# Convolution first, turned copies on GpSimd, and a projection by halves of a chunk, in a four-layer network of scans

## The chip, the cores and the metric

The kernel runs on one core of a Trainium2 chip. The core has a matrix engine (TensorE, PE in the profile; its weight loads are PEld), VectorE (DVE), ScalarE (ACT), GpSimd (POOL) and SyncE (SP, which here only issues DMAs). The metric is the device time of one execution in microseconds. A time "before" is the median of three runs.

## The reference

Four layers, each `x = x + layer(groupnorm(x))` on an image batch of 4 x 64 x 64 x 192 in float32. Layers 0 and 3 are the ones touched. Both are a two-dimensional selective scan; layer 0 has 384 inner channels (DI), layer 3 has 192. Cut to what matters (layer 0):

```python
xz = x @ in_proj_w.T
xp, z = (xz[..., :DI], xz[..., DI:])
xc = silu(depthwise_conv3x3(xp, conv_w) + conv_b)      # channels first, 64 x 64
x0 = xc.reshape(B, DI, L)                              # read by rows, L = 4096
x1 = jnp.swapaxes(xc, 2, 3).reshape(B, DI, L)          # read by columns
xs = jnp.stack([x0, x1, x0[..., ::-1], x1[..., ::-1]], axis=1)
x_dbl = jnp.einsum('bkdl,kcd->bkcl', xs, x_proj_weight)   # 44 rows: 12 step, 16 B, 16 C
dts = jnp.einsum('bkrl,kdr->bkdl', dts_r, dt_projs_weight)
delta = jax.nn.softplus(dts + dt_projs_bias[None, :, :, None])

def step(h, inp):
    u_l, dt_l, Bl, Cl = inp
    dA = jnp.exp(dt_l[..., None] * A[None])
    h = dA * h + (dt_l * u_l)[..., None] * Bl[:, :, None, :]
    y = jnp.sum(h * Cl[:, :, None, :], axis=-1)
    return (h, y)
```

Layer 1 holds four one-dimensional scans along lines of the image, layer 2 a Toeplitz product. The four directions of a scan are added, normalized, gated with `silu(z)` and projected back.

## The kernel before

Layers 0 and 3 run image by image. For each image there are three stages, in pools of memory of their own: `ss2d_input`, `ss2d_scan`, `ss2d_output`.

`ss2d_input` (L430) normalizes the image, then goes through NT tiles of P channels (3 of 128 in layer 0, 2 of 96 in layer 3). For each tile TensorE makes the input projection (`in_ps`, 8 chunks of 512 pixels, L455) and ScalarE copies it into a zero-framed image `pad` (L459). The 3 x 3 convolution follows. For the last tile it is nine TensorE matmuls per chunk with diagonal weights `taps` into `conv_ps` (L472), and ScalarE applies the silu twice, into `o` by rows (L473) and into `by_col` by columns (L474). For the other tiles it is nine VectorE operations on the whole tile (L481, L483), and ScalarE again applies the silu twice (L484, L485). Each tile is stored whole, `o` to `u_d[0]` and `by_col` to `u_d[1]` (L487). There are four PSUM tiles for `in_ps` and `conv_ps`, two buffers of `o` and one of `by_col`.

`ss2d_scan` (L489) takes 32 jobs for an image: four directions of 8 chunks of 512 pixels. A job has units of 64 channels by 4 of the 16 states (two states on each half of the partitions): 24 units in layer 0. `run_jobs` (L104) writes out the order of the units. The preparation of later jobs is put between the units of the running one, at offsets in units that the table `when` gives (L513): load u at -33, project at -29, turn_b at -27, step_size at -21, -19, -17, finish at -15, turn at -13, -11, -9. These steps are in `prepare` (L189):

- `project`: `xd_ps`, three matmuls that add up the 44 rows x 512 (L199), the copy `xd` (L201) and its store to `bc_dram` (L211), from which rows of B and C are read back broadcast.
- `turn_b`: the 16 rows of B turned in four pieces (`b_ps`, L219), copied to `bt` (L221), from which ScalarE makes the diagonal tiles `diag` (L282).
- `step_size(t)`: one matmul with 12 rows of contraction for each tile of 128 channels (`dt_ps`, L225), copied out with a bias into `delta` (L228).
- `finish`: softplus (L232), then on VectorE `dtu` = delta x u (L233). `turn`: `dtu` turned (L242).

The PSUM pool `mm` that these steps use has two tiles of one bank each. A unit has: on TensorE `b` (eight matmuls of 64 x 256, L324), on ScalarE two exponentials `dA` (L347), on VectorE two scans of 512 (L364), on ScalarE a copy of the carried state (L367), on GpSimd the product `hc` with C (L369), and on TensorE the sum over states `y` (two matmuls of 64 x 512, L387). Three units of a job in layer 0 are "direct": their b comes from GpSimd (`bs`, L301) and TensorE makes none. `b` has two PSUM buffers.

The program's order on each engine is settled when it is built, by a scheduler that may move an instruction past others; each engine then runs its list in order, and waits on semaphores. SP issues nearly all DMAs in one list.

Of the kernel before, what the change touches and what calls it, by code (L numbers as in the profile page):

```python
# [7 lines left out]
F32 = mybir.dt.float32  # L8
AF = mybir.ActivationFunctionType
# [4 lines left out]
B, HW, L = 4, 64, 4096  # L14
C = 192
PC, KC = 96, 2
N = 16
R = 12
E = R + 2 * N
T = 512  # L20
NCH = L // T
ROWS = T // HW
PAIRS = N // 4
NB = T // 128
# [12 lines left out]
class Kernel:  # L37
# [151 lines left out]
    def prepare(self, job, pools):  # L189

        nc = self.nc
        prep, mm = pools["prep"], pools["mm"]
        P, NT, DI, w = job["P"], job["NT"], job["DI"], job["w"]

        def project():
            u = job["u"]
            ps = mm.tile([E, T], F32, name="xd_ps", tag="mm")
            for t in range(NT):
                nc.tensor.matmul(ps, w["xw"][:, t, :], u[:, t], start=t == 0, stop=t == NT - 1)  # L199
            xd = job["xd"] = prep.tile([E, T], F32, name="xd", bufs=1)  # L200
            nc.scalar.copy(xd, ps)  # L201
            job["bc"] = self.bcd.tile([2 * N, T], F32, name="bc_dram")
            if job["carry"] is None:

                by_half = job["bc"].rearrange("(a n) l -> a (n l)", n=2).rearrange(
                    "a (h n l) -> h a n l", h=2, n=2
                )
                for h in range(2):
                    nc.scalar.dma_start(by_half[h], xd[0 : 2 * N, h * 256 : (h + 1) * 256])
            else:  # L210
                nc.scalar.dma_start(job["bc"], xd[0 : 2 * N, :])  # L211
            job["delta"] = prep.tile([P, NT, T], F32, name="delta", bufs=1)
            job["dtu"] = prep.tile([P, NT, T], F32, name="dtu", bufs=1)
            job["dtuT"] = prep.tile([128, NB, DI], F32, name="dtuT",)

        def turn_b():
            ps = mm.tile([128, NB, N], F32, name="b_ps", tag="mm")
            for k in range(NB):
                nc.tensor.transpose(ps[:, k, :], job["xd"][0:N, k * 128 : (k + 1) * 128], self.ident[:N, :N])  # L219
            bt = job["bt"] = prep.tile([128, NB, N], F32, name="bt")  # L220
            nc.scalar.copy(bt, ps)  # L221

        def step_size(t):
            dp = mm.tile([P, T], F32, name="dt_ps", tag="mm")
            nc.tensor.matmul(  # L225
                dp, w["dtw"][2 * N : E, t * P : (t + 1) * P], job["xd"][2 * N : E, :], start=True, stop=True
            )
            nc.scalar.activation(job["delta"][:, t, :], dp, AF.Identity, bias=w["dtb"][:, t : t + 1])  # L228
# [201 lines left out]
    def ss2d_input(self, x_in, xn_d, u_d, P, NT, inw, cw, cb):  # L430

        tc, nc = self.tc, self.nc
        S = HW + 2
        with (
# [16 lines left out]
            for t in range(NT):  # L451
                for c in range(NCH):
                    ps = psum.tile([P, T], F32, name="in_ps", tag="mm")
# [6 lines left out]
                        pad[:, t, 1 + c * ROWS : 1 + (c + 1) * ROWS, 1 : 1 + HW],  # L460
                        ps.rearrange("p (a b) -> p a b", b=HW),
                    )
                o = pu.tile([P, HW, HW], F32, name="o")
                by_col = pu.tile([P, HW, HW], F32, name="by_col", bufs=1)
                bias = cb[:, t : t + 1]
                if t == NT - 1:
                    for c in range(NCH):
                        rows = slice(c * ROWS, (c + 1) * ROWS)
                        ps = psum.tile([P, ROWS, HW], F32, name="conv_ps", tag="mm")
                        for j in range(9):  # L470
                            win = pad[:, t, c * ROWS + j // 3 : (c + 1) * ROWS + j // 3, j % 3 : j % 3 + HW]
                            nc.tensor.matmul(ps, taps[:, j, :], win, start=j == 0, stop=j == 8)  # L472
                        nc.scalar.activation(o[:, rows, :], ps, AF.Silu, bias=bias)  # L473
                        nc.scalar.activation(  # L474
                            by_col.rearrange("p b a -> p a b")[:, rows, :], ps, AF.Silu, bias=bias
                        )
                else:
                    for j in range(9):
                        win = pad[:, t, j // 3 : j // 3 + HW, j % 3 : j % 3 + HW]
                        if j == 0:  # L480
                            nc.vector.tensor_scalar_mul(o, win, cw[:, t, 0:1])  # L481
                        else:
                            nc.vector.scalar_tensor_tensor(o, win, cw[:, t, j : j + 1], o, ALU.mult, ALU.add)  # L483
                    nc.scalar.activation(by_col.rearrange("p b a -> p a b"), o, AF.Silu, bias=bias)  # L484
                    nc.scalar.activation(o, o, AF.Silu, bias=bias)  # L485
                for to, of in zip(u_d, (o, by_col)):
                    nc.sync.dma_start(to[:, t, :], of.rearrange("p a b -> p (a b)"))  # L487

    def ss2d_scan(self, pre, u_d, y_d, P, NT, ways, A, dtb):  # L489
        tc, nc, ins = self.tc, self.nc, self.i  # L490
        DI = P * NT
        bufs = dict(c=5, bc=2, diag=5, both=6, dtu2=2) if NT == 3 else dict(c=6, bc=2, diag=6, both=6, dtu2=4)
        with (
# [27 lines left out]
            for k, (col, rev) in sorted(enumerate(ways), key=lambda one: one[1]):  # L521
                w = {"dtb": dtb[:, k, :], "A": A[:, k]}

                def weights(k=k, w=w):
                    w["xw"] = self.load(pw, "xw", ins[f"{pre}x_w"][k])
                    w["dtw"] = pw.tile([E, DI], F32, name="dtw")
                    nc.sync.dma_start(w["dtw"][2 * N : E, :], ins[f"{pre}dt_w"][k])

                for c in range(NCH - 1, -1, -1) if rev else range(NCH):
                    first = not jobs or jobs[-1]["k"] != k  # L530
# [575 lines left out]
```

## Time and profile before

| | |
|---|---|
| median of three runs | 31847.99 us (31831.84 to 31864.97) |
| profiled execution | 31794.9 us, span 31793.1 us |
| PE busy | 28311.3 us (89%) |
| ACT busy | 23362.1 us (73%) |
| POOL busy | 22678.0 us (71%) |
| DVE busy | 22474.8 us (71%) |
| mean granted TensorE clock | 0.948 |
| scans of layer 0, image 0 (from first scan to last) | about 229 to 2530 us |
| input stage of layer 0, image 0 (to the first `xd_ps`) | 0 to 191.6 us |

Layer 0 takes the first 10.8 ms; layer 3 begins at about 25.3 ms. In the lines of the timeline the columns are start, duration, engine, line, operation, result<-operands, shapes and count, and in brackets how long the engine stood idle before it and what ended that. A group of instructions has after the bar its busy time, the mean of one in ns, and the idle time before it with the releasers. A line of busy time by stretch gives the stretch, its length, and for each engine the busy time and the number of instructions.

### The profile page before, as it was taken

How to read it: one execution, taken by the hardware profiler on the slowest of the kernel's cores; microseconds unless marked ns; L12 is line 12 of the kernel's file. 1: busy time of each engine (PE TensorE's matmuls, PEld its weight loads, DVE VectorE, ACT ScalarE, POOL GpSimd, SP SyncE). 2: the span in 40 equal slices, each digit the busy share in tenths (PEclk: the TensorE clock that was granted, in tenths of full speed). 3: DMA queues.
4: the chain of work that ended last, by engine and by line, in shares of the span. 5: the costliest groups of instructions: out<-in, count | busy, mean ns of one | idle time of the engine just before them, and what ended most of it. 6: DMA issues, size and time to landing. Idle time of an engine off the chain costs nothing. (4 is left out here: it accounts for less than half of the span.)

```text
span 31793.1 us, 449637 instructions
## 1 busy us (share of the span) xinstructions
PE 28311.3 (89%) x162840; PEld 13772.2 (43%) x162840; DVE 22474.8 (71%) x16587; ACT 23362.1 (73%) x50239; POOL 22678.0 (71%) x9755
## 2 busy tenths in 40 slices
PE   8997998999899699999999999999588988888888
PEld 4453554454445344444444444444355343434344
DVE  7887887788788677777777777777433267676767
ACT  7885885887688488888888888888133287878788
POOL 6884885888488488888888888888000086767777
PEclk9998999999999899999999999999788999999999
DMA  3333333333333423233333333333533444444444
GB/s 101 100 97 110 99 97 107 103 98 98 109 100 97 135 93 93 93 97 98 98 98 96 95 95 95 98 98 99 132 72 72 109 129 120 128 124 125 124 124 124
DMA packets 1565670, 3326.87 MB, mean 105 GB/s; under 512 B 343781, under 2 KB 356438, under 8 KB 1546934
## 3 DMA queue, kind: packets, MB, share of 16 engines
q1 hardware_dynamic: 1403702, 3021.19, 34.7%
q10 hardware_dynamic: 159744, 276.91, 2.6%
q8 instruction: 1289, 21.12, 0.3%
q14 instruction: 935, 7.66, 0.1%
HBM read 2137.94 MB, written 656.08 MB: 88 GB/s over the span
## 5 line engine op out<-in xcount | busy, mean ns | idle before, releaser
L369 POOL TENSOR_TENSOR hc<-h,c 128x1024 f32<-128x1024 f32 x7680 | 18189.2, 2384 | 3115.9 <-DVE h L364 1317.7
L324 PE MATMUL b<-diag,dtuT 128*64 128x256 f32 x98304 | 12805.9, 391 | 800.1 <-DVE h L364 679.9
L324 PEld LDWEIGHTS b<-diag,dtuT 128*64 128x64 f32 x98304 | 7507.3, 140 | 6835.9 <-issue 3091.1
L387 PE MATMUL y<-hc,fold 128*64 128x512 f32 x30720 | 8995.0, 598 | 587.4 <-POOL hc L369 572.6
L364 DVE TENSOR_TENSOR_SCAN h<-dA,carry,b 128x512 f32<-128x512 f32 x6720 | 8195.0, 1264 | 1805.9 <-PE b L324 1134.3
L347 ACT ACTIVATE dA<-both,A 128x512 f32<-128x512 f32 (+1 forms) x12288 | 8279.8, 711 | 203.0 <-DVE h L357 182.0
L357 DVE TENSOR_TENSOR_SCAN h<-dA,b 128x1024 f32<-128x1024 f32 x2304 | 5251.7, 2284 | 2047.7 <-PE b L324 883.2
L282 ACT ACTIVATE diag<-ident,bt 128x128 f32<-128x128 f32 x20480 | 6527.3, 391 | 124.5 <-ACT b L347 86.1
L301 POOL TENSOR_TENSOR bs<-dtu,bc 128x1024 f32<-128x1024 f32 x1536 | 3638.4, 2369 | 1479.7 <-DMA c<-bc_dram 1087.9
L387 PEld LDWEIGHTS y<-hc,fold 128*64 128x64 f32 x30720 | 2497.6, 138 | 2981.7 <-POOL hc L369 1262.0
L441 POOL MEMSET pad<- 128x13068 f32 (+1 forms) x8 | 73.4, 9177 | 3977.5 <-DMA inw<-in_L_in_w 3004.7
L347 ACT ACTIVATE b<-both,A 128x504 f32<-128x504 f32 (+1 forms) x3072 | 2078.1, 676 | 412.7 <-DVE h L364 379.8
L357 DVE TENSOR_TENSOR_SCAN h<-b,bs 128x1024 f32<-128x1024 f32 x768 | 1754.1, 2284 | 659.6 <-ACT b L347 391.2
L367 ACT COPY carry<-h 128x2 f32<-128x2 f32 x4608 | 851.4, 185 | 1367.1 <-DVE h L364 1165.5
L364 DVE TENSOR_TENSOR_SCAN h<-b,carry,bs 128x512 f32<-128x512 f32 x1344 | 1638.0, 1259 | 105.7 <-POOL hc L369 95.3
L364 DVE TENSOR_TENSOR_SCAN h<-dA,b 128x512 f32<-128x512 f32 x960 | 1112.9, 1205 | 436.2 <-ACT dA L347 175.8
L347 ACT ACT_TABLE_LOAD x1018 | 1306.1, 1283 | 15.0 <-ACT b L335 0.3
L730 PE MATMUL in_ps<-xn,in_w 96*128 96x512 f32 x1536 | 933.4, 738 | 329.4 <-DMA xn<-m_row 177.8
L747 DVE SCALAR_TENSOR_TENSOR u<-in_ps,conv_w,u 128x504 f32<-128x504 f32 (+2 forms) x1152 | 835.7, 725 | 460.3 <-ACT u L742 438.6
L233 DVE TENSOR_TENSOR dtu<-delta,u 128x1536 f32<-128x1536 f32 (+1 forms) x256 | 611.4, 2388 | 758.2 <-ACT delta L232 602.9
L242 PEld LDWEIGHTS dtu_ps<-ident,dtu 128*128 128x128 f32 (+1 forms) x4096 | 422.1, 142 | 875.7 <-issue 569.3
L730 PE MATMUL z_ps<-xn,in_w 96*128 96x512 f32 x1536 | 761.7, 618 | 0.0
(155 smaller groups left out, 22077.8 us busy)
## 6 DMA issues: line engine op xcount, KB each, us to landing
c<-bc_dram SPq DMA_DIRECT2D x3072, 256.0 KB
both<-delta SPq DMA_DIRECT2D x2048, 128.0 KB
bc<-bc_dram SPq DMA_DIRECT2D x768, 256.0 KB
both<-delta_dram SPq DMA_DIRECT2D x768, 256.0 KB
dtu<-dtu_dram SPq DMA_DIRECT2D x768, 256.0 KB
dtu<-dtu SPq DMA_DIRECT2D x1280, 128.0 KB
L_y<-out ACTq DMA_DIRECT2D x512, 256.0 KB
u<-L_u SPq DMA_DIRECT2D x160, 768.0 KB
```

The costliest lines, as they stand in the source:

```text
L233: (nc.gpsimd if job["carry"] is None else nc.vector).tensor_mul(job["dtu"], delta, job["u"])
L282: nc.scalar.activation(to, self.ident, AF.Copy, scale=of)
L301: self.nc.gpsimd.tensor_mul(by(b), dtu, by(job["bbc"][p]))
L324: nc.tensor.matmul(to, job["dtuT"][:, k, g * 64 : (g + 1) * 64], job["diag"][p][:, k, 2 * q : 2 * q + 2, :], start=True, stop=True,)
L347: nc.scalar.activation(to[n], of, AF.Exp, scale=w["A"][:, g, 2 * p + n : 2 * p + n + 1])
L357: nc.vector.tensor_tensor_scan(h[:, way], dA[:, way], b[:, way], 0.0, ALU.mult, ALU.add)
L364: nc.vector.tensor_tensor_scan(hn[:, n, way], dA[:, n, way], by_n[:, n, way], start, ALU.mult, ALU.add)
L367: nc.scalar.copy(carry[g, p], hn[:, :, 0 if rev else T - 1])
L369: nc.gpsimd.tensor_mul(hc, h, job["cbc"][p])
L387: nc.tensor.matmul(y[c * 64 : (c + 1) * 64, :], self.fold, of, start=first == 0 and n == 0, stop=last == LAST and n == 1)
L730: nc.tensor.matmul(ps, w["in_w"][:, k, to + t * P : to + (t + 1) * P], job["xn"][:, k, :], start=k == 0, stop=k == KC - 1,)
L747: nc.vector.scalar_tensor_tensor(u[:, :, to], ps[:, :, of], tap(3 - j), u[:, :, to], ALU.mult, ALU.add)
```

## The change

In `ss2d_input` the loop over tiles is split: first all input projections and copies into `pad`, then the convolutions, beginning with the last tile, TensorE's. ScalarE now applies the silu once; the copy by columns is made from its result by GpSimd. In TensorE's tile each chunk goes to a small tile `one` and is stored by itself; in the others the first chunk (8 rows) is finished and stored ahead of the rest. `by_col` has two buffers.

In `prepare`, for jobs of layer 0 alone (`halves`), `project` computes the two halves of a chunk's 512 pixels on two halves of the output rows (0-43 and 64-107), so that `xd` is 128 x 256; the 44 columns of the weights are filled up with zeros to 64. `bc_dram` is written by two DMAs; `turn_b` turns two pieces of 128 x 128; `step_size` makes two matmuls of 256 pixels, from rows 32-43 and from rows 96-107, into two PSUM tiles, each copied out by itself. For this the weights of `dt` are loaded twice, at two row positions, and `xw` gets a memset on GpSimd, in layer 3 too.

```diff
+        halves = job["carry"] is not None and NT == 3
         def project():
             u = job["u"]
-            ps = mm.tile([E, T], F32, name="xd_ps", tag="mm")
-            for t in range(NT):
-                nc.tensor.matmul(ps, w["xw"][:, t, :], u[:, t], start=t == 0, stop=t == NT - 1)
-            xd = job["xd"] = prep.tile([E, T], F32, name="xd", bufs=1)
+            if halves:
+                ps = mm.tile([128, 256], F32, name="xd_ps", tag="mm")
+                for t in range(NT):
+                    for h in range(2):
+                        nc.tensor.matmul(
+                            ps[h * 64 : (h + 1) * 64, :], w["xw"][:, t, :], u[:, t, h * 256 : (h + 1) * 256],
+                            start=t == 0, stop=t == NT - 1,
+                        )
+                xd = job["xd"] = prep.tile([128, 256], F32, name="xd", bufs=1)
...
+            elif halves:
+                by_half = job["bc"].rearrange("a (h l) -> h a l", h=2)
+                for h in range(2):
+                    nc.scalar.dma_start(by_half[h], xd[h * 64 : h * 64 + 2 * N, :])
...
         def turn_b():
+            if halves:
+                ps = mm.tile([128, 2, 128], F32, name="b_ps", tag="mm")
+                for k in range(2):
+                    nc.tensor.transpose(ps[:, k, :], job["xd"][:, k * 128 : (k + 1) * 128], self.ident)
+                of = ps.rearrange("p k (h e) -> p k h e", h=2)[:, :, :, 0:N]
+                nc.scalar.copy(bt.rearrange("p (h k) n -> p k h n", h=2), of)
+                return
...
         def step_size(t):
+            if halves:
+                parts = []
+                for h in range(2):
+                    parts.append(mm.tile([P, 256], F32, name="dt_ps", tag="mm"))
+                    rows = slice(h * 64 + 2 * N, h * 64 + E)
+                    nc.tensor.matmul(
+                        parts[h], w["dtw"][rows, t * P : (t + 1) * P], job["xd"][rows, :], start=True, stop=True
+                    )
+                for h in range(2):
+                    to = job["delta"][:, t, h * 256 : (h + 1) * 256]
+                    nc.scalar.activation(to, parts[h], AF.Identity, bias=w["dtb"][:, t : t + 1])
+                return
...
-                o = pu.tile([P, HW, HW], F32, name="o")
-                by_col = pu.tile([P, HW, HW], F32, name="by_col", bufs=1)
+            for t in [NT - 1, *range(NT - 1)]:
+                by_col = pu.tile([P, HW, HW], F32, name="by_col")
+                turned = by_col.rearrange("p b a -> p a b")
                 bias = cb[:, t : t + 1]
...
-                        nc.scalar.activation(o[:, rows, :], ps, AF.Silu, bias=bias)
-                        nc.scalar.activation(
-                            by_col.rearrange("p b a -> p a b")[:, rows, :], ps, AF.Silu, bias=bias
-                        )
+                        one = pu.tile([P, ROWS, HW], F32, name="one")
+                        nc.scalar.activation(one, ps, AF.Silu, bias=bias)
+                        nc.gpsimd.tensor_copy(turned[:, rows, :], one)
+                        nc.sync.dma_start(u_d[0][:, t, c * T : (c + 1) * T], one.rearrange("p a b -> p (a b)"))
...
-                    nc.scalar.activation(by_col.rearrange("p b a -> p a b"), o, AF.Silu, bias=bias)
-                    nc.scalar.activation(o, o, AF.Silu, bias=bias)
-                for to, of in zip(u_d, (o, by_col)):
-                    nc.sync.dma_start(to[:, t, :], of.rearrange("p a b -> p (a b)"))
+                    for rows in (slice(0, ROWS), slice(ROWS, HW)):
+                        nc.scalar.activation(o[:, rows, :], o[:, rows, :], AF.Silu, bias=bias)
+                        nc.sync.dma_start(
+                            u_d[0][:, t, rows.start * HW : rows.stop * HW],
+                            o[:, rows, :].rearrange("p a b -> p (a b)"),
+                        )
+                    nc.gpsimd.tensor_copy(turned, o)
+                nc.sync.dma_start(u_d[1][:, t, :], by_col.rearrange("p a b -> p (a b)"))
...
-                    w["xw"] = self.load(pw, "xw", ins[f"{pre}x_w"][k])
-                    w["dtw"] = pw.tile([E, DI], F32, name="dtw")
-                    nc.sync.dma_start(w["dtw"][2 * N : E, :], ins[f"{pre}dt_w"][k])
+                    w["xw"] = pw.tile([P, NT, 64], F32, name="xw")
+                    nc.gpsimd.memset(w["xw"][:, :, E:64], 0.0)
+                    nc.sync.dma_start(w["xw"][:, :, 0:E], ins[f"{pre}x_w"][k])
+                    w["dtw"] = pw.tile([128, DI], F32, name="dtw")
+                    for h in range(2):
+                        nc.sync.dma_start(w["dtw"][h * 64 + 2 * N : h * 64 + E, :], ins[f"{pre}dt_w"][k])
```

In the built program the order on each engine stays as it was for layers 1 and 2. In an input stage of layer 0 ScalarE's list is now: the 24 copies into `pad`, three chunks of the last tile, tile 0, three chunks, tile 1, two chunks. SP's list ends with the turned tile 1, the last chunk, the turned last tile, the weights and u.

More of the change, by code (lines that the diff above doesn't have):

```diff
@@ L193, in prepare @@
         P, NT, DI, w = job["P"], job["NT"], job["DI"], job["w"]
+        halves = job["carry"] is not None and NT == 3
         def project():
             u = job["u"]
-            ps = mm.tile([E, T], F32, name="xd_ps", tag="mm")
-            for t in range(NT):
-                nc.tensor.matmul(ps, w["xw"][:, t, :], u[:, t], start=t == 0, stop=t == NT - 1)
-            xd = job["xd"] = prep.tile([E, T], F32, name="xd", bufs=1)
+            if halves:
[7 more added lines that the diff above has]
+                xd = job["xd"] = prep.tile([128, 256], F32, name="xd", bufs=1)
+            else:
+                ps = mm.tile([E, T], F32, name="xd_ps", tag="mm")
+                for t in range(NT):
+                    nc.tensor.matmul(ps, w["xw"][:, t, 0:E], u[:, t], start=t == 0, stop=t == NT - 1)
+                xd = job["xd"] = prep.tile([E, T], F32, name="xd", bufs=1)
             nc.scalar.copy(xd, ps)
@@ L216, in turn_b @@
         def turn_b():
+            bt = job["bt"] = prep.tile([128, NB, N], F32, name="bt")
+            if halves:
[5 more added lines that the diff above has]
+                return
             ps = mm.tile([128, NB, N], F32, name="b_ps", tag="mm")
@@ L219, in turn_b @@
                 nc.tensor.transpose(ps[:, k, :], job["xd"][0:N, k * 128 : (k + 1) * 128], self.ident[:N, :N])
-            bt = job["bt"] = prep.tile([128, NB, N], F32, name="bt")
             nc.scalar.copy(bt, ps)
         def step_size(t):
+            if halves:
[10 more added lines that the diff above has]
+                return
             dp = mm.tile([P, T], F32, name="dt_ps", tag="mm")
@@ L472, in ss2d_input @@
                             nc.tensor.matmul(ps, taps[:, j, :], win, start=j == 0, stop=j == 8)
-                        nc.scalar.activation(o[:, rows, :], ps, AF.Silu, bias=bias)
-                        nc.scalar.activation(
-                            by_col.rearrange("p b a -> p a b")[:, rows, :], ps, AF.Silu, bias=bias
-                        )
+                        one = pu.tile([P, ROWS, HW], F32, name="one")
+                        nc.scalar.activation(one, ps, AF.Silu, bias=bias)
+                        nc.gpsimd.tensor_copy(turned[:, rows, :], one)
+                        nc.sync.dma_start(u_d[0][:, t, c * T : (c + 1) * T], one.rearrange("p a b -> p (a b)"))
                 else:
+                    o = pu.tile([P, HW, HW], F32, name="o")
                     for j in range(9):
```

## Prediction

> **What bounds the kernel now.** I read four views: busy time by stretch, to see which engine fills the scans of layer 0; groups of instructions in 500 to 2300 us (25 chunks of image 0), for counts and durations; the timeline of TensorE in one chunk, for what a step costs in place; and the timelines of ScalarE and TensorE through an input stage.
>
> Busy time by stretch:
>
> ```profile
> core 0: us, PE busy (x) PEld busy (x) DVE busy (x) ACT busy (x) POOL busy (x), PEclk, DMA share, GB/s
> 500.00:2300.00 1800.00, 1698.44 (x11440) 900.24 (x11438) 1536.32 (x1257) 1505.62 (x3692) 1578.72 (x673) 0.97 0.38 99
> ```
>
> Per chunk (divide by 25): 72.0 us, with TensorE 67.9 busy, GpSimd 63.1, VectorE 61.5, ScalarE 60.2. TensorE is the bound; the next engine has 8.9 us to spare. Its missing 4.1 us come once a chunk:
>
> ```profile
> L324 PE MATMUL b<-diag,dtuT 128*64 128x256 f32 x8356 | 1079.1, 393 | 101.6 <-DVE h L364 101.4
> L233 DVE TENSOR_TENSOR dtu<-delta,u 128x1536 f32<-128x1536 f32 x25 | 76.8, 3072 | 27.0 <-ACT delta L232 27.0
> ```
>
> 101.6 / 25 = 4.1 us of waiting for the scans: VectorE puts the 3.07 us product dtu between two scans, after 1.1 us of waiting for delta, and both PSUM buffers of b are then full.
>
> What a step costs, in place:
>
> ```profile
> 1224.51 1.89 PE L387 MATMUL y<-hc,fold 128*64 128x512 f32 x8
> 1226.23 2.31 PE L199 MATMUL xd_ps<-u,xw 128*44 128x512 f32 x5
> ...
> 1251.58 1.06 PE L387 MATMUL y<-hc,fold 128*64 128x512 f32 x4
> 1252.44 1.93 PE L324 MATMUL b<-diag,dtuT 128*64 128x256 f32 x16
> 1254.16 1.06 PE L387 MATMUL y<-hc,fold 128*64 128x512 f32 x4
> 1255.15 1.12 PE L225 MATMUL dt_ps<-xd,dtw 12*128 12x512 f32 x2
> 1256.20 1.95 PE L324 MATMUL b<-diag,dtuT 128*64 128x256 f32 x16
> 1257.98 1.03 PE L387 MATMUL y<-hc,fold 128*64 128x512 f32 x4
> ```
>
> A float32 matmul is two records. From start to start, eight products of b (256 columns each, in pairs on output rows 0-63 and 64-127) take 1.72 us, 0.43 a pair; two y (512 columns) take 0.86 together. So two halves of the output rows run at once. The projection xd has one half only: three matmuls of 512 columns at 0.86 are 2.58 us. One dt matmul takes 0.99 + 1.05 + 1.78 less the undisturbed 0.86 + 1.72 = 1.24 us, 0.86 of it streaming and 0.38 the change to and from its shape.
>
> The input stage of image 0:
>
> ```profile
> 78.13 31.07 PE L472 MATMUL conv_ps<-pad,taps 128*128 128x512 f32 x72
> 141.91 33.21 PE L472 MATMUL conv_ps<-pad,taps 128*128 128x512 f32 x72 [32.71 <-ACT by_col L474]
> 191.61 5.32 PE L199 MATMUL xd_ps<-u,xw 128*44 128x512 f32 x6 [16.49 <-DMA u<-L_u]
> ...
> 109.27 7.46 ACT L484 ACTIVATE by_col<-o,cb 128x4096 f32<-128x4096 f32 x1 [29.05 <-DVE o L483]
> 127.22 7.19 ACT L484 ACTIVATE by_col<-o,cb 128x4096 f32<-128x4096 f32 x1 [6.76 <-DVE o L483]
> ```
>
> The convolution on TensorE is half done at 109.2, then stands for 32.7 us: four PSUM tiles are full, and ScalarE waits in order for VectorE and writes the turned copies (7.2 to 7.5 us each, 3.7 for the straight ones). After it ends, 16.5 us pass until u has been stored and loaded.
>
> **What the Trainium skill says.** "TensorEngine Tiling (Array Packing)", Key Properties: tiles of the array run independently, while a change of tiling mode drains it. The trace agrees on both: 0.43 us for a pair, and 0.38 us around a dt step. "TensorE: Matmul & The Clock Gate", Why this matters for your kernels: contractions of few rows placed in different row groups run concurrently (four tiles measured 3.07 times faster). In this trace only a hint: at 197.73 a matmul of b_ps (rows 0-15) and at 197.74 one of dt_ps (rows 32-43) start together. "GPSIMD Engine Reference", 8. Key points: GpSimd shares its SBUF interfaces with VectorE when VectorE reads two SBUF inputs. The trace agrees: dtu takes 1.76 us at 204.89 with GpSimd idle, 3.07 beside it.
>
> **The change, part by part.**
>
> *xd by halves* (layer 0, 4 images x 32 = 128 chunks). Three matmuls become six of 64x256 in pairs, the shape of b: 3 x 0.43 = 1.29 instead of 2.58. Saved: 1.29 us of TensorE per chunk.
>
> *b_ps.* Four turns of 16 rows cost 0.49 in place (start of b_ps 1234.07, b 1234.41, plus 0.15 around). Two of 128x128: four such (dtu) cost 0.74 in place, 0.43 of it streaming, so two cost 0.52. Nothing either way.
>
> *dt by halves.* Per step, two matmuls of 256 columns in row groups 32 and 96, to two PSUM tiles. If concurrent, 0.43 + 0.38 instead of 1.24: 0.43 saved, three times a chunk: 1.29. If serial, 0. I take concurrent, on the page and the hint.
>
> *ScalarE.* Each dt leaves two evictions of 256 instead of one of 512. Between 0.39 (128 columns) and 0.67 (512) I take 0.45 each: +0.23 x 3 = +0.7; the copy of xd falls from 0.56 to about 0.4; one DMA issue more (0.33 us, beside other work in the trace). ScalarE goes from 60.2 to about 61, hidden in a period near 70. But the last dt eviction stands before the softplus that dtu waits for: +0.25 us, and in the built order a copy of carry, which waits for a scan, stands between its halves. I charge 0.4 us a chunk (0 to 0.8), which lengthens the stall of TensorE.
>
> Each dt step now fills both tiles of the pool mm. Evictions follow their matmul by about 1.7 to 2.2 us (1255.15 to 1257.33) and the next user comes 6.4 us later: no wait.
>
> Scan: 1.29 + 1.29 - 0.4 = 2.2 us x 128 = 282 us. Nothing else is late before that: a period of 69.8 stands above GpSimd's 63.1 and VectorE's 61.5.
>
> *Input stage, layer 0.* With ScalarE only emptying PSUM between, TensorE runs on: 72 products x 0.86 from 78.1 end at 140.0, the last silu at 140.7. VectorE's convolutions end at 127.2 and now have GpSimd's copies beside them, 7168 elements by then. A copy is not in the trace: at least the memset's rate (13068 in 10.99 us, 0.84 ns), at most that of the product hc (1024 in 2.37, 2.3 ns). So 6 to 16 us of GpSimd, of which VectorE loses part; I take 4 (0 to 16): 131. Then silu of this tile, 4 us, 135; its turned copy 5.5 us (3.4 to 9.4), 140.5; the last chunk's copy, 142. SP has in order the 2 MB store of this turned tile, the last chunk, the 2 MB store of the last turned tile, the weights (one DMA more each, 0.4), then u at about 143.5. The stores ran at 419 GB/s: 5 us each, from 140.5 to 150.7, then u with 0.8 MB and about 2 us of latency: xd at about 155 instead of 191.6. I take 36 us saved, 21 (copy and contention at their worst) to 42 (u not queued behind the stores). Times 4: 144.
>
> *Input stage, layer 3.* There TensorE is in front too: its convolution starts at 27004.81, waits 11.8, and xd comes at 27097.8, 9 us of that waiting for the last whole-tile store. Unbroken it ends at 27066.6; silu, copy, a 1.6 MB store (3.8 us) and u lead to about 27077. Saved 20 us (15 to 24), times 4: 80. Layer 3's scan keeps its matmuls; its weights gain a memset and one small DMA, long before use.
>
> Layers 1 and 2 have the same instructions in the same order.
>
> Sum: 282 + 144 + 80 = 506 us. Against the profiled execution (31794.9): 31289. The median of the runs is 53 us above that one, so 31848 - 506 = 31342.
>
> **Rivals.**
> 1. *Row groups do not overlap for float32.* For it: yt_ps uses two quadrants at once and still takes 21.4 us for 192 products of 64 columns, 0.11 each, which is serial streaming (or the rate of issue). Against: the hint above. Scan 0.9 x 128 = 115: 115 + 224 = 339, 31509.
> 2. *Another engine sets the scan.* GpSimd has direct units with two products (4.74 us) in a row, and VectorE catches up only where TensorE has extra work, which is what goes. Then only the input stages gain: 31848 - 224 = 31624. Against: 6 to 8 us of slack a chunk.
> 3. *The input stages give nothing,* because turned copies, VectorE's slowdown and 4 MB of stores end as late as before. It needs about 36 us of delay in each: 31848 - 282 = 31566.
> 4. *Slower.* TensorE, in order, waits in each dt step for both tiles of mm to be emptied, since ScalarE waits for scans between. At one unit (2.6 us) a step, 7.8 - 2.6 = 5.2 us a chunk, x 128 = 666, less 224: 32290. It decides above a stall of 1.6 us a step (224/128 = 1.75, plus 2.6 of gain, plus the 0.5 of the bound below, over 3). The built order puts evictions close behind, which speaks against.
>
> **How the numbers follow.** Forecast 0.52; rivals 1 to 4: 0.20, 0.10, 0.06, 0.12. The likeliest's own range is 31255 to 31440. For 8 in 10 it must reach over rivals 1 and 3 and the edge of 2: 31250 to 31610. About 64 us (0.2%) is what a measurement can tell from no change. Rivals 1 to 3 are all faster; of rival 4 I put 0.10 beyond 64 us slower and 0.02 within, so faster 0.87 with some of 2 lost to 0.01 of no change: faster 0.87, same 0.03, slower 0.10.
>
> **What would show it.** xd's six matmuls should take 1.29 us from first start to the next b; a dt step 0.81 in place (1.24 if rival 1); a chunk of layer 0 69.8 us; no new wait of dt_ps for delta; the convolution in one piece, and xd at about 155 in image 0. It is wrong if TensorE's busy time falls but the chunk stays near 72, or if u lands after 175.

## The result, and the profile after

The changed kernel takes 31516.71 us, the median of four runs (31496.9 to 31527.75); the kernel before, in the same comparison, 31839.92 us (31803.57 to 31864.97). The ratio is 0.9899, with a 95% interval of 0.9882 to 0.9916: 323 us less, where 506 were forecast. The profiled execution fell from a span of 31793.1 us to 31495.0.

Where the 298 us between the two profiled spans lie is read from landmarks on TensorE: the first matmul of layer 1 (`in_ps<-xn`) and the first of layer 3 (`in_ps<-x`).

| | before | after | difference |
|---|---|---|---|
| layer 0 ends (first matmul of layer 1) | 10991.4 us | 10743.7 us | -247.7 |
| layers 1 and 2 | 14365 | 14396 | +31 |
| layer 3 | 6436.7 | 6355.0 | -81.7 |
| layer 0: first `in_ps` to first `xd_ps`, mean of the four images | 157.6 | 131.3 | -26.3 each |
| layer 0: distance of two `dtu` products on VectorE | 72.27 | 71.1 | -1.17 each |

Layers 1 and 2 have the same instructions in both kernels, and in all kernels of this study they took between 14349 and 14441 us: a difference of 50 us there is nothing. Of the 248 us of layer 0, 4 x 26.3 = 105 lie in the input stages and the other 143 in the scans.

First the busy time by stretch, of the changed kernel, for the stretch shown of before and for one short stretch that matters later (columns: stretch, its length, then busy time and instructions of PE, PEld, DVE, ACT and POOL, the granted TensorE clock, and the DMA's share and rate):

```profile
1232.40:1235.80 3.40, 3.40 (x16) 2.17 (x18) 2.19 (x2) 2.26 (x6) 3.40 (x3) 0.50 0.91 237
...
500.00:2300.00 1800.00, 1662.02 (x11884) 914.62 (x11882) 1560.26 (x1280) 1536.44 (x3834) 1601.82 (x687) 0.96 0.38 100
```

A chunk now takes 71.1 us, so 1800 us hold 25.3 chunks. TensorE is busy 65.7 us a chunk instead of 68.2: the change took 2.5 us of work from it, as meant. The chunk fell by 1.17 only. The groups of instructions tell what took the rest:

```profile
L360 PE MATMUL b<-diag,dtuT 128*64 128x256 f32 x8494 | 1063.0, 393 | 138.0 <-DVE h L400 137.0
...
L269 DVE TENSOR_TENSOR dtu<-delta,u 128x1536 f32<-128x1536 f32 x26 | 78.1, 3004 | 29.9 <-ACT delta L268 29.9
```

TensorE waits 137.0 us for VectorE's scans where it waited 101.4: 5.4 us a chunk instead of 4.1. One chunk on TensorE's timeline, of the changed kernel:

```profile
1227.02 0.66 PE L278 MATMUL dtu_ps<-ident,dtu 128*128 128x128 f32 x4
1232.39 3.68 PE L360 MATMUL b<-diag,dtuT 128*64 128x256 f32 x16 [4.72 <-DVE h L400]
1235.83 1.56 PE L423 MATMUL y<-hc,fold 128*64 128x512 f32 x4
1237.21 1.91 PE L360 MATMUL b<-diag,dtuT 128*64 128x256 f32 x16
...
1255.06 1.46 PE L203 MATMUL xd_ps<-u,xw 128*64 128x256 f32 x12
1256.62 1.95 PE L360 MATMUL b<-diag,dtuT 128*64 128x256 f32 x16
...
1276.27 0.70 PE L253 MATMUL dt_ps<-xd,dtw 12*128 12x256 f32 x4
1278.02 1.95 PE L360 MATMUL b<-diag,dtuT 128*64 128x256 f32 x16 [1.04 <-DVE h L400]
...
1282.35 1.06 PE L423 MATMUL y<-hc,fold 128*64 128x512 f32 x4
1283.34 0.70 PE L253 MATMUL dt_ps<-xd,dtw 12*128 12x256 f32 x4
1283.97 1.95 PE L360 MATMUL b<-diag,dtuT 128*64 128x256 f32 x16
1285.74 1.03 PE L423 MATMUL y<-hc,fold 128*64 128x512 f32 x4
```

Read from start to start. The projection now takes 1256.62 - 1255.06 = 1.56 us to the next b (2.58 before). A dt step takes 1285.74 - 1282.35 = 3.39, less the undisturbed 0.86 + 1.72, so 0.81 in place (1.24 before). Two stops of TensorE in a chunk of the kernel before, for comparison:

```profile
1177.17 1.95 PE L324 MATMUL b<-diag,dtuT 128*64 128x256 f32 x16 [0.36 <-DVE h L364]
...
1198.68 0.66 PE L242 MATMUL dtu_ps<-ident,dtu 128*128 128x128 f32 x4
1199.27 1.07 PE L387 MATMUL y<-hc,fold 128*64 128x512 f32 x2
1204.07 3.81 PE L324 MATMUL b<-diag,dtuT 128*64 128x256 f32 x17 [3.73 <-DVE h L364]
```

The first stop stands behind a direct unit and the first dt step. It was 0.36 us and is now 1.04 (at 1278.02). VectorE, for which TensorE waits there, is busy from 1267.50 on without a break:

```profile
1267.50 7.43 DVE L400 TENSOR_TENSOR_SCAN h<-dA,carry,b 128x512 f32<-128x512 f32 x6 [0.65 <-ACT dA L383]
1274.85 0.66 DVE L598 TENSOR_TENSOR out<-y,earlier 128x512 f32<-128x512 f32 x1
1275.43 2.44 DVE L400 TENSOR_TENSOR_SCAN h<-dA,carry,b 128x512 f32<-128x512 f32 x2
1277.79 2.43 DVE L400 TENSOR_TENSOR_SCAN h<-b,carry,bs 128x512 f32<-128x512 f32 x2
```

The second, behind the turned product, is listed with 4.72 us instead of 3.73, but it did not get longer. From the start of the turned product to the next b it takes 1232.39 - 1227.02 = 5.37 us, and 1204.07 - 1198.68 = 5.39 before. In the kernel before a y runs inside the stop (at 1199.27), in 12 of 24 chunks; in the changed kernel it stands behind the stop in TensorE's list, in all 25. So the longer listed wait is a y that moved out of it. What was really kept and lost shows in the distances between such fixed points of TensorE's list (means of 24 to 26 chunks of image 0):

| from start to start | before | after | difference |
|---|---|---|---|
| first turned product to the b behind the long stop | 5.05 | 5.06 | +0.01 |
| that b to the second turned product | 7.20 | 7.44 | +0.24 |
| second turned product to the projection | 15.16 | 15.16 | 0 |
| projection to the turned B | 7.84 | 6.71 | -1.13 |
| turned B to the first dt step | 14.28 | 14.57 | +0.29 |
| first dt step to the second | 6.62 | 6.75 | +0.13 |
| second dt step to the third | 6.37 | 5.95 | -0.42 |
| third dt step to the first turned product | 9.82 | 9.40 | -0.42 |

The projection saves 1.13 us and each dt step should save 0.42, together 2.4. Of this, 0.55 are lost behind the first dt step, 0.29 in the stretch before it and 0.24 behind the long stop, where that y now runs; 1.3 are kept in this image.

Behind the long stop is another loss, which the kernel before had as well. Eight products of b, 1.72 us elsewhere, take 1235.83 - 1232.39 = 3.44 us there, the two y after them 1237.21 - 1235.83 = 1.38 us instead of 0.86, and the first stretch above shows the clock of TensorE at 0.50 in just this time.

The input stage of image 0, on the timelines of TensorE, GpSimd, VectorE and SyncE's queue:

```profile
79.11 61.97 PE L509 MATMUL conv_ps<-pad,taps 128*128 128x512 f32 x144
165.54 2.83 PE L203 MATMUL xd_ps<-u,xw 128*64 128x256 f32 x12 [24.45 <-DMA u<-L_u]
...
103.29 4.76 POOL L512 COPY by_col<-one 128x512 f32<-128x512 f32 x1 [4.69 <-ACT one L511]
123.56 15.29 POOL L512 COPY by_col<-one 128x512 f32<-128x512 f32 x3
141.96 7.08 POOL L529 COPY by_col<-o 128x4096 f32<-128x4096 f32 x1 [3.11 <-ACT o L524]
148.90 1.04 POOL L512 COPY by_col<-one 128x512 f32<-128x512 f32 x1
...
70.56 67.35 DVE L521 SCALAR_TENSOR_TENSOR o<-pad,cw,o 128x4096 f32<-128x4096 f32 x13
...
149.07 0.32 SPq L530 DMA_DIRECT2D L_u<-by_col  x1
155.42 2.71 SPq L60 DMA_DIRECT2D u<-L_u  x2
```

The convolution on TensorE runs in one piece and ends at 141.1 us. VectorE's ends at 137.9; before, the same 13 operations took 57.6 us and ended at 127.2. GpSimd copies 128 x 512 in 1.04 us when alone (148.90), in 4.76 beside VectorE's convolution (103.29), and later takes 15.29 for three: the two engines slow each other. Then SP's queue waits for the turned copy (141.96 + 7.08 = 149.04), goes through stores and weights, and comes to u at 155.42.

### The profile page after: what moved, and what is told of

It is laid out like the page before. It is cut to its first block, busy times and chain, and to the rows that moved or that the text cites. A ratio compares the mean times of both kernels' runs of the same rounds, so it can differ in the third digit from the quotient of the medians.

```text
span 31495.0 us, 452842 instructions
## 1 busy us (share of the span) xinstructions
PE 28016.1 (89%) x164120; PEld 13777.8 (44%) x164120; DVE 22496.5 (71%) x16587; ACT 23230.4 (74%) x50559; POOL 22921.2 (73%) x9863
## 4 chain that ended last, share of the span: by engine, by line
PE 39%; DVE 14%; POOL 14%; ACT 13%; DMA 10%; issue 7%; SPq 2%; ACTq 0%; DVEq 0%; POOLq 0%
PE b L360 16%; POOL hc L405 11%; DVE h L400 8%; PE y L423 8%; ACT diag L318 5%; ACT dA L383 4%; DVE h L393 3%; DMA xn<-m_col 3%; DMA xn<-m_row 2%; PE in_ps L777 2%; POOL bs L337 2%; SPq L325 2%; PE yt_ps L1014 2%; PE conv_ps L509 2%; DMA xn<-t_xn 2%
## 5 line engine op out<-in xcount | busy, mean ns | idle before, releaser
L360 PE MATMUL b<-diag,dtuT 128*64 128x256 f32 x98304 | 12662.5, 392 | 955.3 <-DVE h L400 829.9
L423 PE MATMUL y<-hc,fold 128*64 128x512 f32 x30720 | 8832.2, 601 | 579.8 <-POOL hc L405 566.2
```

Of the source, the lines that this page charges most:

```text
L360: nc.tensor.matmul(to, job["dtuT"][:, k, g * 64 : (g + 1) * 64], job["diag"][p][:, k, 2 * q : 2 * q + 2, :], start=True, stop=True,)
L423: nc.tensor.matmul(y[c * 64 : (c + 1) * 64, :], self.fold, of, start=first == 0 and n == 0, stop=last == LAST and n == 1)
```

## The experiments

The twelve kernels below are edits of the changed kernel. "Chunk" is the distance of two `dtu` products in layer 0; "wait" is TensorE's waiting of b for VectorE's scans, from the view of waits in 500 to 2280 us, divided by the chunks in it; "slow clock" is what the b products behind stops of 2 us and more took over 1.74 us, per chunk, from the timeline of TensorE (b alone; other matmuls behind the stop can be slow too). "Wait" counts a y that runs inside a stop as work, so it grows when a y moves out of a stop. The jobs that the `halves` branch takes are those of layer 0 alone, 4 x 32 = 128 chunks; where an expectation says "layers 0 and 3" for such an edit, layer 0 is what it changes.

| kernel | time, us | layer 0 ends | chunk | wait | slow clock |
|---|---|---|---|---|---|
| before | 31840 | 10991 | 72.27 | 4.0 | 1.5 |
| after | 31517 | 10744 | 71.1 | 5.3 | 1.6 |
| e1_input_only | 31654 | 10888 | 72.27 | - | 1.6 |
| e2_xd_only | 31542 | 10813 | 71.6 | 4.4 | 1.3 |
| e3_one_evict | 31487 | 10720 | 71.0 | 4.8 | 1.1 |
| e4_split_dtu | 31594 | 10864 | 72.1 | 6.5 | 1.7 |
| e5_turned_act | 31462 | 10712 | 71.1 | - | - |
| e6_stores_off_sp | 31457 | 10747 | 71.2 | - | - |
| e7_early_xd | 31351 | 10570 | 69.7 | 4.9 | 1.0 |
| e8_third_dtu | 31303 | 10558 | 69.6 | 4.3 | 1.1 |
| e9_fill | 31302 | 10558 | 69.5 | 3.1 | 0.3 |
| e10_act_in_stop | 31277 | 10473 | 69.0 | 5.0 | 0.4 |
| e11_act_in_stop_turn | 31219 | 10455 | 69.0 | 4.6 | 0.5 |
| e12_all | 31154 | 10386 | 68.3 | 3.1 | 0.1 |

The times of e1 to e11 are of one execution each, beside which the kernel before took 31827 to 31831 us; e12 is a median of five.

**The parts apart.** First the input stages without the scan's edits:

```diff
-        halves = job["carry"] is not None and NT == 3
+        halves = False
```

> The new input stages alone; projection, turn of B and dt as in the kernel before. Additive parts: a chunk of layer 0 stays at 72.3 us (distance of two dtu products on VectorE), each first xd in layer 0 comes about 26 us earlier after its in_ps than before, in layer 3 about 18 to 20, total about 31840 - 105 - 80 = 31655. If the parts depend on each other (the padded weights or the two row positions cost something in the input stage), the first xd moves by several us against the changed kernel.

Measured: 31654.09 us, the chunk at 72.27 as before, layer 0 shorter by 103.6. The two parts of the change add up; each image's input stage is worth 26 us whatever the scan does.

Then the projection by halves alone, with `xd` copied back to 44 x 512 and the rest of the preparation as before:

```diff
+        whole = True
...
+                xd = job["xd"] = prep.tile([E, T], F32, name="xd", bufs=1)
+                for h in range(2):
+                    nc.scalar.copy(xd[:, h * 256 : (h + 1) * 256], ps[h * 64 : h * 64 + E, :])
...
-            if halves:
+            if halves and not whole:
```

> The changed kernel with the projection by halves, but xd copied back to 44 x 512 by two ScalarE copies, and turn of B and dt whole as before. TensorE has 1.0 us less per chunk than before (1.56 instead of 2.58 for xd). Theory A, every microsecond taken from TensorE shortens the chunk: 71.3 us per chunk. Theory B, TensorE's gain is partly given back as waiting for VectorE's scans: 71.6 to 71.9, and the wait of b for the scans grows from 4.1 us a chunk.

Measured: 31541.91 us, chunk 71.55 to 71.80 in the four images. The projection takes 1.02 us less of TensorE and the chunk keeps 0.65 of it; the wait rises by 0.4. So one edit alone already gives a third of its gain back as waiting for VectorE. The long stop kept its length here too (5.02 us from the turned product to b); the stretch from the turned B to the first dt step grew from 14.28 to 14.73 us, and the first dt step, which is not changed in this kernel, from 6.62 to 6.78.

**Is it ScalarE's second eviction?** The prediction put its charge of 0.4 us down to it. Here both dt matmuls go to one PSUM tile of two banks, and one eviction of 512 takes both:

```diff
-                    parts.append(mm.tile([P, 256], F32, name="dt_ps", tag="mm"))
+                two = mm.tile([P, 2, T], F32, name="dt_ps", tag="mm")[:, :, 0:256]
...
-                for h in range(2):
-                    to = job["delta"][:, t, h * 256 : (h + 1) * 256]
-                    nc.scalar.activation(to, parts[h], AF.Identity, bias=w["dtb"][:, t : t + 1])
+                to = job["delta"][:, t, :].rearrange("p (h l) -> p h l", h=2)
+                nc.scalar.activation(to, two, AF.Identity, bias=w["dtb"][:, t : t + 1])
```

> The changed kernel with both halves of dt in one PSUM tile of two banks, copied out by one ScalarE instruction of 512 as before (pool mm then has one such tile instead of two single ones). Theory S, ScalarE's doubled evictions delay dA, the copies of carry and the softplus and so took the missing 1.0 us of gain: the chunk goes from 71.1 to about 70.1 us and the waits of the scans for dA fall back from 2.3 to about 0.8 us a chunk. Theory V, VectorE's stop for dtu in front of a direct unit takes it whatever ScalarE does: 70.8 to 71.2.

Measured: 31487.36 us, chunk 70.73 to 71.19. It gains some 0.2 us a chunk, so the evictions are at most a small part of the loss. The places of the loss did not change: the first dt step to the second takes 6.77 us (6.75 in the changed kernel) and the turned B to the first dt step 14.57, as there; the gain lies behind the long stop (7.00 instead of 7.44 us), since in 13 of 25 chunks of this kernel a y runs inside the stop again. Theory S had a second sign, and it failed as well: in 500 to 2280 us the scans wait 72.1 us for dA, 2.9 a chunk, where the changed kernel has 59.0 (2.4) and the kernel before 19.1 (0.8). Why they wait longer for ScalarE than before was not tried; it stays open how much of VectorE's lateness comes from there.

**Does the product need to be one piece?** `dtu` in three pieces, so that scans can come between:

```diff
-            (nc.gpsimd if job["carry"] is None else nc.vector).tensor_mul(job["dtu"], delta, job["u"])
+            if halves:
+                return
...
+        def product(t):
+            nc.vector.tensor_mul(job["dtu"][:, t, :], job["delta"][:, t, :], job["u"][:, t, :])
...
+                3: dict(... finish=-15, product=(-15, -13, -11),
```

> The changed kernel with the product dtu in three pieces of one tile each, due two units apart, so that VectorE's stop of 3.1 us is broken up. Theory V (the stop fills both PSUM buffers of b and TensorE then stands, 5.3 us a chunk): the wait of b for scans falls by 1 us or more and the chunk to 70 us or less. Theory S: the stop is only where ScalarE's delay shows, the chunk stays at 70.8 to 71.2.

Measured: 31593.79 us, slower than the changed kernel; chunk 72.1, wait 6.5. The expected shorter stop did not come. On VectorE's timeline two pieces (2.65 us at 1238.09), one unit of scans and the third piece (0.66 at 1243.63) all still stand before the two scans that TensorE waits for; the stop is 4.86 us in that chunk and up to 6.4 in others. It is the total ahead of those scans that counts.

**How much is VectorE's product worth?** This kernel leaves out two of the three tiles of the product (the first tile stands in for them):

```diff
+            if halves:
+                nc.vector.tensor_mul(job["dtu"][:, 0, :], delta[:, 0, :], job["u"][:, 0, :])
...
-                    ps[:, k, :], job["dtu"][:, t, k * 128 : (k + 1) * 128], self.ident[:P, :P]
+                    ps[:, k, :], job["dtu"][:, 0 if halves else t, k * 128 : (k + 1) * 128], self.ident[:P, :P]
```

> Leaves out two of the three tiles of the product delta*u in layers 0 and 3 (the first tile's product stands in for them, with the same transposes and copies). Theory V: VectorE is held up 2.05 us less at the product, TensorE's stop there falls from 4.4 to about 2.4 us, and the clock after it recovers: chunk 68.5 to 69.3 us in layer 0, 31240 to 31340 us in all. Theory R: chunk falls by less than 1 us (70.3 or more).

Measured: 31303.4 us, chunk 69.4 to 69.7, a gain of 1.5 us where the product lost 2.05. That decides against theory R (less than 1 us): VectorE's product stands on the path. But it falls a little short of theory V's 68.5 to 69.3. From the turned product to the next b it takes 4.01 us instead of 5.06, and from there to the second turned product 6.77 instead of 7.44. The slow clock behind the stop stayed at 1.1 of 1.6 us, since stops of 2.7 to 3.7 us remain. This says what the stop is worth; it does not say that the change made it longer, which the distances above exclude.

**Moving TensorE's own work toward the stop.** The same instructions, the projection ten units earlier:

```diff
-                3: dict(load=-33, project=-29, turn_b=-27, step_size=(-21, -19, -17), finish=-15,
+                3: dict(load=-43, project=-39, turn_b=-37, step_size=(-21, -19, -17), finish=-15,
```

(The tiles of delta and dtu, which `project` allocated, are allocated in the first dt step instead.)

> The changed kernel with the projection of each chunk ten units earlier, so that its six matmuls, and two units later the transposes of B, stand on TensorE's queue just where it waits for VectorE's product delta*u. Same instructions. Theory V (the chunk is TensorE's work plus its stop for VectorE at that product): the stop of 4.4 us a chunk falls by the 1.5 to 2 us that now fill it, and the chunk falls from 71.1 to 69.2 to 69.8 us: 31300 to 31400 us. Theory R (the bound has gone to VectorE or ScalarE as a whole, and TensorE only waits for it): the stop falls and other short stops rise by the same, chunk 70.8 to 71.3, time within 50 us of the changed kernel's.

Measured: 31350.8 us, chunk 69.6 to 69.9, as theory V had it. But not for its reason alone: the wait fell by 0.4 us a chunk only, and the slow clock by 0.6. In the trace the projection stands one unit ahead of the stop; only the transposes of B are in it. And behind the direct unit where the projection stood before, TensorE now waits some 1.4 us at a time for VectorE's scans (1.2 us a chunk; none there in the changed kernel): work taken from that place turned into waiting there.

**The clock.** So the slow matmuls behind the stop were tested by themselves. This kernel takes nothing away and adds 20 transposes of the identity behind the first turned product, into a PSUM tile that nobody reads:

```diff
             nc.scalar.copy(job["dtuT"][:, :, t * P : (t + 1) * P], ps)
+            if halves and t == 0:
+                ps = mm.tile([128, NB, P], F32, name="fill_ps", tag="mm")
+                for k in range(20):
+                    nc.tensor.transpose(ps[:, k % NB, :], self.ident, self.ident)
```

> Adds 20 transposes of the identity matrix, which nobody reads, to TensorE's queue behind the first tile's turned product in layers 0 and 3: 3.3 us of work (4 such take 0.66) in the stop of 4.72 us that stands there now. Work is added, none is taken away. Theory C (the b matmuls after the stop take 3.44 us instead of 1.72 because TensorE stood idle and its clock was lowered): the stop shrinks to about 1.4 us, the b after it takes 1.7 to 1.9 us, and the chunk falls by 1.4 to 1.8 us, from 71.1 to 69.3 to 69.7: 31270 to 31330 us, less time with more work. Theory N (the slow matmuls belong to the place, not to the idleness): b after the stop stays at 3.4, chunk 70.9 to 71.3, 31470 to 31530 us.

Measured: 31302.49 us, 214 less than the changed kernel's median with more work, chunk 69.5. TensorE's timeline of this kernel, at the same place in a chunk:

```profile
1277.06 0.66 PE L278 MATMUL dtu_ps<-ident,dtu 128*128 128x128 f32 x4
1277.56 2.35 PE L285 MATMUL fill_ps<-ident 128*128 128x128 f32 x20
1282.44 1.95 PE L364 MATMUL b<-diag,dtuT 128*64 128x256 f32 x16 [2.54 <-DVE h L404]
1284.19 1.06 PE L427 MATMUL y<-hc,fold 128*64 128x512 f32 x4
```

The 20 transposes took 2.35 us, not 3.3, so 2.54 us of the stop are left.

Busy time by stretch, of the same kernel, for the idle rest of the stop and for the matmuls behind it:

```profile
1279.90:1282.40 2.50, 0.00 (x1) 0.00 (x0) 2.50 (x4) 2.35 (x5) 2.27 (x1) 1.00 0.87 241
1282.40:1285.80 3.40, 3.35 (x28) 2.38 (x30) 3.40 (x4) 2.32 (x6) 3.40 (x3) 1.00 0.85 252
```

The clock stays at 1.00, and b takes 1284.19 - 1282.44 = 1.75 us instead of 3.44. DMA traffic is as high as in the stretch at clock 0.50 of the changed kernel (0.85 against 0.91), so it is the idleness and not the transfers beside it. Theory N is refuted. The shorter wait (3.1 us a chunk) is only the fill's own time counted as work. The gain of 1.6 us a chunk is the slow clock that went: 1.3 us in b, and the rest in the y behind it. Counted with the clock records of the trace over all of TensorE's busy time, the half clock cost 2.2 us a chunk in the changed kernel and 0.6 here.

**The input stage.** The turned copies on ScalarE again, otherwise as changed:

```diff
-                        nc.gpsimd.tensor_copy(turned[:, rows, :], one)
+                        nc.scalar.activation(turned[:, rows, :], ps, AF.Silu, bias=bias)
...
-                    nc.gpsimd.tensor_copy(turned, o)
+                    nc.scalar.copy(turned, o)
```

> The changed kernel with its turned copies back on ScalarE; all else as changed. Theory G (GpSimd's copies beside VectorE stretch the convolution of layer 0 from 127.2 to 137.9 us, and that sets the first projection): VectorE's convolution of image 0 ends at about 127 us, and TensorE's own convolution, which ends at 141.1, comes to set the stage; first projection at 152 to 155 instead of 165.5, so 10.5 to 13.5 us less for each image of layer 0, up to 5 for each of layer 3: 31430 to 31475 us. Theory Q (the queue behind the convolution sets it: turned stores and weights in SP's queue): the convolution is shorter but the first projection stays at 162 or later, and the time is within 20 us of the changed kernel's.

Measured: 31462.42 us. VectorE's convolution ends at 127.6 us, u is issued at 146.95 and xd comes at 156.42, 9.1 us earlier; layer 0 is 31.8 us shorter, layer 3 the same (6355.6 us). Theory Q is out (162 or later). Theory G had the direction and the cause right, but its 152 to 155 us for the first projection were a little too early. The turned copies are better off on ScalarE; the change's order of work pays without GpSimd in it. Of the 34.5 us between the two profiled spans 31.8 lie in layer 0.

The other theory, the queue, by taking the turned stores off SP:

```diff
-                nc.sync.dma_start(u_d[1][:, t, :], by_col.rearrange("p a b -> p (a b)"))
+                nc.gpsimd.dma_start(u_d[1][:, t, :], by_col.rearrange("p a b -> p (a b)"))
...
-                    nc.gpsimd.memset(w["xw"][:, :, E:64], 0.0)
+                    nc.vector.memset(w["xw"][:, :, E:64], 0.0)
```

> The changed kernel with its turned stores issued by GpSimd instead of SyncE, and the clearing of the spare columns of x_w on VectorE. GpSimd's copies stay. Theory G: VectorE's convolution still ends near 138 us, but the chunk loads no longer wait in SP's queue for the last turned copy (149.07): the first projection of image 0 at 153 to 157, so 8 to 12 us less for each image of layer 0, and at most as much in layer 3; 31450 to 31490 us. Theory Q: the whole of the lost 10.5 us and more returns, first projection at 150 or earlier. If neither, the projection stays at 165 and the time at 31500 to 31515: then the load waits for something else than SP's queue.

Measured: 31456.74 us, inside the range of theory G, with xd at 153.49 as it said. It would be wrong to book that as a gain: the time is in the range by luck. Layer 0 ends at 10747 us, 3 later than in the changed kernel; the 40 us less come from layers 1 and 2, which have no edit and took 14349 us here, 47 less than in the changed kernel's profile. ScalarE's timeline of this kernel shows where the 12 us of the earlier projection went:

```profile
158.77 0.47 ACT L258 ACTIVATE delta<-dt_ps,dtb 128x256 f32<-128x256 f32 x1 [0.59 <-PE dt_ps L253]
165.64 0.40 ACT L318 ACTIVATE diag<-ident,bt 128x128 f32<-128x128 f32 x1 [6.39 <-DMA dtw<-in_L_dt_w]
```

The profile puts this wait down to a load of `dtw`, 18 KB, while the 2 MB stores are under way; whether it is this load or another was not tried. Of 12 us, 4 are left at the first dtu product (173.15 us instead of 177.40), and none at the end of the layer.

**Put together.** Turned copies on ScalarE, and the projection two units later than in e7, directly behind the first turned product:

```diff
-                3: dict(load=-33, project=-29, turn_b=-27, step_size=(-21, -19, -17), finish=-15,
+                3: dict(load=-41, project=-37, turn_b=-33, step_size=(-21, -19, -17), finish=-15,
```

> The turned copies on ScalarE, and the projection of the next chunk two units later than in the kernel that put it ten units earlier: its six matmuls then stand directly behind the first turned product, in the stop itself. Theory V+C: the stop of 4.7 us shrinks to about 3.1, and if TensorE is then not idle for long enough to lose its clock, the b after it takes 1.7 us: chunk 68.9 to 69.6 us, layer 0 some 35 us less again for the input stages: 31230 to 31320 us. Theory R (VectorE and ScalarE set the chunk now): 69.6 to 69.9 as with the projection ten units earlier, 31310 to 31350 us.

Measured: 31276.69 us, chunk 69.0: theory V+C. The stop is now 3.28 us and shorter, and behind it the clock mostly holds (8 of 27 stops of 2 us and more are followed by slow matmuls, 25 of 26 in the changed kernel).

Then the third turned product six units later as well (`turn=(-13, -11, -5)`):

> As the one before, and the third tile's turned product moved six units later, into the short stop of TensorE (1.4 us) after the third direct unit. Theory V+C: that stop takes 0.66 us of work that stood on the path: chunk 68.4 to 69.1 us, 31160 to 31260 us. Theory R: no change against the one before, within 25 us.

Measured: 31219.28 us, but the chunk stays at 69.0. Layer 0 is 17.5 us shorter and layers 1 and 2, untouched, 41. Of this edit theory R was right: the short stop that it was meant for became 0.6 us shorter (1.38 in e7's trace, 0.80 here), and nothing came of it.

Last, 12 transposes of the identity behind the projection, in the same PSUM tile:

```diff
+                full = mm.tile([128, T], F32, name="xd_ps", tag="mm")
+                ps = full[:, 0:256]
...
+                for k in range(12):
+                    at = 256 + k % 2 * 128
+                    nc.tensor.transpose(full[:, at : at + 128], self.ident, self.ident)
```

> The kernel before this one (turned copies on ScalarE, projection in the stop, third turned product later), and behind the projection 12 transposes of the identity that nobody reads, 1.4 us, in the stop of 3.3 us that is left. Theory C (what is left to gain there is the lowered clock: 11.5 us of slow matmuls in 1780 us, 0.45 a chunk): the stop falls to about 1.9 us, no b matmul group of twice its time stays, chunk 68.5 to 68.8 us, 31150 to 31200 us, 2.0 to 2.2% less than before. Theory R (VectorE and ScalarE set the chunk; the fill only changes what TensorE does while it waits): chunk 68.9 to 69.2, 31200 to 31290 us, ratio to before 0.980 to 0.983.

Measured: 31153.51 us, median of five (31123.88 to 31199.76), against 31843.2 for the kernel before; ratio 0.9787, interval 0.9774 to 0.9801. The chunk is 68.3 us, better than theory C had it. Its busy time by stretch:

```profile
500.00:2300.00 1800.00, 1714.53 (x12644) 993.08 (x12645) 1617.79 (x1333) 1585.37 (x3974) 1659.10 (x713) 1.00 0.39 104
```

The granted clock is 1.00, and no stop of 2 us or more is left from 500 to 2280 us. This version beats both kernels: 363 us below the changed kernel's median.

## Why the prediction was right, and where its sum was off

- *TensorE bounds the scan, and its work falls by 2.6 us.* Right: 2.5 less busy (68.2 to 65.7). The dt step was forecast at 0.81 us in place and takes 0.81; row groups do overlap for float32, so rival 1 falls. The projection was forecast at 1.29 and takes 1.56. The turned B costs 0.55 against 0.49: nothing, as said.
- *"I charge 0.4 us a chunk (0 to 0.8), which lengthens the stall of TensorE."* This is the term that was mis-sized, and its mechanism was wrong. The stall behind the product did not lengthen (5.05 and 5.06 us), and with the doubled evictions taken away (e3) the loss stays where it was. What was given back is 1.1 us a chunk, half of it (0.55 us) behind the first dt step; another 0.24 is the y that left the stop. At the first dt step a direct unit stands: TensorE has no b to do for it and less other work than before, so it comes sooner to a VectorE that is busy without a break. So 128 x 1.17 is about 150 us instead of 282. Work taken from those stretches turns in part into waiting: 0.4 of 1.02 us in e2, and in e7 the projection left a wait of 1.2 us where it had stood. That was rival 2's argument, with VectorE as the other engine and at half its strength; the average slack of 6 to 8 us a chunk, which spoke against it, is slack elsewhere in the chunk.
- *Nothing new waits for the two tiles of `mm`.* Right; TensorE shows no wait for evictions of that size, and rival 4 falls.
- *Input stage, layer 0: 36 us an image, xd at about 155.* 26 us, xd at 165.5. The convolution in one piece was right to 1.1 us (141.1 against 140.0). What was mis-sized is the copies: "VectorE loses part; I take 4", and VectorE lost 10.7; the turned copy was taken at 5.5 us and takes 7.1. Together that is 8 of the 10 us. e5, with no GpSimd copies, gives 9.1 of them back. Rival 3 falls.
- *Input stage, layer 3: 20 us an image.* The first projection comes 18.4 us earlier after its first `in_ps` (124.1 before, 105.7 after, means of the four images), and layer 3 is 81.7 us shorter, against 80.
- *The size.* The error is 128 x (2.2 - 1.17) = 132 us in the scans and about 40 in the input stages, together 172 of the 183. So the measured 31516.71 us lies outside the likeliest's own range (31255 to 31440) and inside the stated one only because that was widened for the rivals. That it falls on rival 1's figure (31509) is chance: what rival 1 says did not happen.

Not seen at all was that the stall, known from the profile, costs twice: once as waiting and once as matmuls at half clock. It was already so before (1.9 us a chunk over all of TensorE's busy time, 2.2 after), so it hardly entered the sum; but it shows in the trace of before, as a b group of 3.81 us (at 1204.07), and was worth more than any part of the change to the scan.

## What to carry to other kernels

Work taken from the engine that bounds a loop counts only as far as no other engine uses that stretch to catch up: count it against the stalls of the loop, not against the average slack. Measure a stop from one fixed point of the loop to another; the listed wait also moves when a neighbour's work moves in or out of it. Where TensorE has a stop of more than 2 us in every round, move work of its own into the stop, or even work for nobody, since in these runs its clock fell while it waited. And time a part by its own landmarks: untouched layers moved by more here than some edits.

## What the runs showed of the hardware

- TensorE's clock is halved by a stop, not by what runs beside it. Behind stops of 3.8 to 4.7 us 25 of the changed kernel's 26 groups of b were slow (3.0 to 3.4 us for 1.72); behind stops of 2.4 to 3.2 us 16 of 26 in e7; and behind stops of 2.2 to 2.6 us 9 of 14 in e9 took over 2 us, 5 of them over 2.4. In e12, with no stop of 2 us in the chunks, the clock is 1.00.
- The half clock comes in whole steps. Between 500 and 2300 us the changed kernel's clock records have 26 spells at 0.50; each lasts 3.41 or 6.83 us, and all begin on one grid of 3.41 us. The Trainium skill, "TensorE: Matmul & The Clock Gate", Part 1, has half rate after an idle window of about 3.4 us that runs freely. The grid agrees. That the window must be idle throughout does not: a stop of 2.2 us cannot hold one. Whether a stop of 2 to 3 us is punished seems to hang on where it falls on the grid, which no run here tests by itself.
- GpSimd's copy of 128 x 512 with a turned output took 1.04 us alone and 1.4 to 5.1 beside VectorE's convolution, whose operations rose from 4.43 us (57.61 / 13) to 5.18 on average, and fell back to 4.43 when the copies went to ScalarE (e5). Both pay.
- Two float32 matmuls with 12 rows of contraction, in row groups that begin at 32 and 96, run at the same time: 0.81 us in place for the pair, where one of twice the columns took 1.24 (the change to and from the shape included).
